# y written in the place of x, a reworked root chain, and the last channels packed in two pairs

## The chip, the cores and the metric

One core of one Trainium2 chip runs the kernel. The metric is device time in microseconds of one execution. The kernel before takes 917.46 us, the median of three runs (916.84 to 920.22).

## The reference

Two layers follow each other on x of shape 4 x 64 x 256 x 256, in float32.

```python
hx = _implicit_filter(z, Xw1, ..., t, deltas)          # 256 taps for each of 64 channels
hy = _implicit_filter(z, Yw1, ..., t, deltas)
k = jnp.einsum('ijk,imk->ijmk', hx, hy)[0]             # a separable 256 x 256 filter for each channel
y = irfft2(rfft2(x) * rfft2(k) / fft_size)[..., :L, :L]
x = y + x * bias[:, None, None]

x1 = transpose(x, (1, 0, 2, 3)).reshape(64, -1)
x1_s = x1[:, ::9]                                      # every ninth pixel
mean1 = mean(x1_s)
cov = x1_s @ x1_s.T / x1_s.shape[1] + 0.01 * eye(64)
deconv = _isqrt_newton_schulz(cov, 5)                  # Y, Z: T = 0.5(3I - ZY); Y = YT; Z = TZ
out = deconv @ (x1 - mean1)
```

The second layer needs the whole first layer before its first output pixel: the 64 x 64 inverse root depends on samples of every image and channel.

## The kernel before, in words

**Convolution.** The filter is separable and causal, so each channel is two multiplications by a triangular Toeplitz matrix, one for each axis. `steps` (L107) has 32 steps, each of eight channels (group g) of one image n; the last sixteen go image by image with groups 6 and 7. A step has four items of two channels. `group(first, second)` (L380) runs the first multiplication of one item and the second multiplication of the item two places before it as 80 interleaved matmuls on PE (L214). ACT then copies the first results from PSUM (L395), and DVE forms y = x * bias + PSUM (L398). `pack` gives DVE some copies under a mask (L312), which gather every ninth pixel of a finished step into `samp[n]`. `store` (L406) issues two DMAs of 256 KB on SP's queue, from the y tile to the DRAM tensors `y_d`. `load_x` (L100) brings x two steps ahead in four DMAs of 512 KB. `half_group` runs the first two and the last two items, for which only one of the two multiplications is left.

**Buffers.** The pool `big` holds four tiles of 16 KB a partition: two with tag "in" for x and two with tag "out" for y. `epool` has two more, `spool` the four `samp`, `tpool` three Toeplitz tiles: 13 tiles in all.

**Covariance.** `covariance(n)` (L320) is 58 matmuls over `samp[n]`. Those of images 0 to 2 stand between convolution groups. For the last four channels of the last step, 18 matmuls with a row-picking matrix (`pack_by_pe`, L288) take the place of the masked copies. Image 3's covariance follows.

**Root.** From L504 on: the 128 x 65 sum is folded to 64 x 64, A's Frobenius norm is taken through two square roots on ACT with a correction on DVE, A is scaled, and five Newton-Schulz rounds follow, each with up to three 64 x 64 products. PE, DVE and ACT alternate. W (the scaled root, repeated for both halves of the partitions) and `shift` (minus the root times the mean) come out.

**Apply.** Finished images are in `y_d` as 32 pieces of 2 MB. `load_y` (L345) brings a piece into one of 13 `homes` (L340), the tiles above, as soon as a tile's last use is over: `early` (L371) puts eight of these loads between convolution steps, five follow after the last store (L469). Each piece is multiplied by W on PE (L580), moved back to its tile by ACT (L585) and DVE (L588), which add `shift`, and written to `out` by DMAs on POOL's queue (L593): four of 512 KB for the first two and the last two pieces, one of 2 MB for the others. A home is loaded again when its piece has been written.

The order of instructions on PE, SP, DVE, ACT and POOL is the order of the program text inside `manual_schedule` (L419 to L470). The root and the apply stage stand outside it. Each queue runs in order; SP's and POOL's issue a DMA only when its buffers are free, and each reuses eight landing semaphores in turn.

Of the kernel before, what the change touches and what calls it, by code (L numbers as in the profile page):

```python
# [37 lines left out]
F32 = mybir.dt.float32  # L38
I32 = mybir.dt.int32
AF = mybir.ActivationFunctionType  # L40
ALU = mybir.AluOpType
# [7 lines left out]
CG = 8  # L49
# [16 lines left out]
def conv_whiten_kernel(ctx: ExitStack, tc: tile.TileContext, a: dict, out: bass.AP):  # L66
# [1 line left out]
    x = a["x"]  # L68

    const = ctx.enter_context(tc.tile_pool(name="const", bufs=1))  # L70
    big = ctx.enter_context(tc.tile_pool(name="big", bufs=2))
    epool = ctx.enter_context(tc.tile_pool(name="epool", bufs=2))
    spool = ctx.enter_context(tc.tile_pool(name="spool", bufs=NB))
    tpool = ctx.enter_context(tc.tile_pool(name="tpool", bufs=3))
# [7 lines left out]

    scratch = big.tile([P, 16, L], F32, tag="out", name="scratch")

    zw = scratch[0:EMB, 13:15, :].rearrange("p a w -> p (a w)")[:, 0 : L + P]
    nc.sync.dma_start(out=zw, in_=a["zw"])
# [18 lines left out]
    steps = [(g, n) for g in range(C // CG - 2) for n in range(NB)]  # L107
    steps += [(g, n) for n in range(NB) for g in range(C // CG - 2, C // CG)]

    x_tiles = [big.tile([P, CG, H2, L], F32, tag="in", name=f"x{u}") for u in range(2)]  # L110
    for c in range(0, CG, 2):
        load_x(x_tiles[0], *steps[0], c)

# [145 lines left out]

    def half_group(item, which):  # L260

        g, n, c, xt, yt, o1s = item
        jobs = []
        for u in range(2):
            banks = [
                psA.tile([P, L], F32, tag="psA", name=f"ph{which}_{g}_{n}_{c + u}_{m}")
                for m in range(H2)
            ]
            jobs.append((banks, (o1s[u] if which else xt[:, c + u]), toep[g][:, which, c + u, :]))
        toeplitz_alone(jobs, which)  # L270
        if which == 0:
            for u in range(2):
                o1s.append(o1pool.tile([P, H2, L], F32, tag="o1", name=f"o1_{g}_{n}_{c + u}"))
        for m in range(H2):
            for u in range(2):
                ps = jobs[u][0][m]
                if which == 0:
                    copy = nc.vector.tensor_copy if u else nc.scalar.copy
                    for to, fr in ((slice(0, HP), slice(HP, P)), (slice(HP, P), slice(0, HP))):
                        copy(o1s[u][to, m], ps[fr])  # L280
                else:
                    ch = g * CG + c + u
                    nc.vector.scalar_tensor_tensor(  # L283
                        yt[:, c + u, m], xt[:, c + u, m], bias[:, ch : ch + 1], ps,
                        ALU.mult, ALU.add,
                    )

    def pack_by_pe(g, n, yt, cs):  # L288
# [12 lines left out]
                )  # L301
        dst = samp[n][:, :, :, g * CG + cs.start : g * CG + cs.stop]
        nc.scalar.copy(dst[:, 0], pk[:, 0].rearrange("p c j -> p j c"))  # L303
        nc.vector.tensor_copy(dst[:, 1], pk[:, 1].rearrange("p c j -> p j c"))

    def pack_ops(g, n, yt, cs):
        def op(s):
# [12 lines left out]
    def covariance(n):  # L320
# [17 lines left out]


    homes = [  # L340
        {"t": (tpool, "toep"), "s": (spool, "samp"), "i": (big, "in"), "o": (big, "out"), "e": (epool, "extra")}[k]
        for k in "eetssitsoiots"
    ]

    def load_y(i):  # L345
# [22 lines left out]
            k = first + (part * 12 // 8 if g < C // CG - 2 else part)  # L368
            blocks[k // 4, k % 4 * 2] = (g, part)

    early = {(26, 4): 1, (26, 6): 1, (27, 4): 1, (28, 2): 1, (29, 6): 1, (31, 4): 2, (31, 6): 1}  # L371
    orders = [list(range(L // HP)), list(reversed(range(L // HP)))]

    def pack(time=math.inf):
# [5 lines left out]
    def group(first, second):  # L380

        units = []
        g1, n1, c1, x1, _, o1s1 = first
        g2, n2, c2, x2, y2, o1s2 = second
        for u in range(2):
            job2 = (bank(f"p2_{g2}_{n2}_{c2 + u}"), o1s2[u], toep[g2][:, 1, c2 + u, :])
            job1 = (bank(f"p1_{g1}_{n1}_{c1 + u}"), x1[:, c1 + u], toep[g1][:, 0, c1 + u, :])
# [4 lines left out]
        for u in range(2):  # L392
            o1 = o1pool.tile([P, H2, L], F32, tag="o1", name=f"o1_{g1}_{n1}_{c1 + u}")
            for to, fr in ((slice(0, HP), slice(HP, P)), (slice(HP, P), slice(0, HP))):
                nc.scalar.copy(o1[to], units[u][0][0][fr])  # L395
            o1s1.append(o1)
            ch = g2 * CG + c2 + u
            nc.vector.scalar_tensor_tensor(  # L398
                y2[:, c2 + u], x2[:, c2 + u], bias[:, ch : ch + 1], units[u][1][0],
                ALU.mult, ALU.add,  # L400
            )

# [1 line left out]
        store(second)  # L404

    def store(second):  # L406
        g, n, c, _, yt, _ = second
        last = (g, n) == steps[-1]
        for b in range(H2):
            row = b * C + g * CG + c  # L410
# [3 lines left out]
            )  # L414
        if last and c == CG // 2 - 2 or not last and c == CG - 2:
            todo.extend(pack_ops(g, n, yt, slice(0, c + 2)))

    engines = mybir.EngineType
    with tc.manual_schedule(  # L419
# [7 lines left out]
        for c in range(0, CG, 2):  # L427
            load_x(x_tiles[1], *steps[1], c)
        for i, (g, n) in enumerate(steps):
            xt = x_tiles[i % 2]  # L430
            yt = big.tile([P, CG, H2, L], F32, tag="out", name=f"y_{g}_{n}")
            for c in range(0, CG, 2):
                item = (g, n, c, xt, yt, [])
                if g == C // CG - 1 and n > 0 and c == 4:
                    covariance(n - 1)
                if len(pending) == 2:
# [4 lines left out]
                if i == 0 and c == 6:  # L441

                    fold = const.tile([P, C], F32, tag="fold", name="fold")
                    nc.vector.tensor_tensor(fold, ident[:, 0:C], ident[:, C:P], ALU.add)
                    twice = const.tile([C, 2, C], F32, tag="twice", name="twice")
                    for u in range(2):
                        nc.vector.tensor_copy(twice[:, u], ident[0:C, 0:C])

                j, cj = i - (c < 4), (c - 4) % CG
                if 0 <= j < len(steps) - 2:  # L450
                    load_x(x_tiles[j % 2], *steps[j + 2], cj)
                if (i, c) in blocks:
                    tg, part = blocks[i, c]
                    if part == 0:
# [2 lines left out]
                    load_toeplitz(toep[tg], tg, part // 4, part // 2 % 2, lo, lo + CG // 2)  # L457
                for _ in range(early.get((i, c), 0)):
                    load_next()
        g, n, c, xt, yt, _ = pending[0]  # L460
        for item in pending:
            half_group(item, 1)
            pack(1.0)
            store(item)

        pack()
        pack_by_pe(g, n, yt, slice(CG // 2, CG))
        covariance(NB - 1)
        while len(loaded) < len(homes):  # L469
            load_next()  # L470


    spare = {}
    for i in range(2):
        t = o1pool.tile([P, H2 * L], F32, tag="o1", name=f"chain{i}")
        for j in range(5):
            spare[5 * i + j] = t[0:C, 72 * j + 72 : 72 * j + 72 + C]
    ones = spare[9]
    nc.gpsimd.memset(ones, 1.0)  # L479
    i15 = spare[8]  # L480
    nc.vector.tensor_scalar(i15, ident[0:C, 0:C], 1.5, None, ALU.mult)
    spots = {"A": [0], "sq": [1], "Y": [2, 3], "T": [4, 5], "Z": [6, 7], "Zs": [1]}

    columns = [t[0:C, 440 + k : 441 + k] for k in range(H2 * L - 440)]

    def column():
        return columns.pop()

    def matrix(tag):
        spots[tag].append(spots[tag].pop(0))  # L490
        return spare[spots[tag][-1]]

    def product(lhsT, rhs, name):
        p = psA.tile([lhsT.shape[1], rhs.shape[1]], F32, tag="psA", name=name)
        nc.tensor.matmul(p, lhsT=lhsT, rhs=rhs, start=True, stop=True)  # L495
        return p

    def keep(p, name, tag):
        t = matrix(tag)
        nc.vector.tensor_copy(t, p)  # L500
        return t


    pd = product(fold, cov, "pd")  # L504
    A = matrix("A")
    nc.vector.scalar_tensor_tensor(A, ident[0:C, 0:C], EPS, pd[:, 0:C], ALU.mult, ALU.add)
    mean = column()
    nc.scalar.copy(mean, pd[:, C : C + 1])

    def root(v, name):  # L510

        s0 = column()
        nc.scalar.activation(s0, v, AF.Sqrt)  # L513
        r = column()
        nc.vector.reciprocal(r, s0)
        s1 = column()
        nc.vector.scalar_tensor_tensor(s1, v, r, s0, ALU.mult, ALU.add)
        s2 = column()
        nc.vector.tensor_scalar(s2, s1, 0.5, None, ALU.mult)
        return s2  # L520

    sq = matrix("sq")
    nc.vector.tensor_tensor(sq, A, A, ALU.mult)
    rowsum = column()
    nc.vector.tensor_reduce(rowsum, sq, AX.X, ALU.add)
    ssq = column()
    nc.vector.tensor_copy(ssq, product(ones, rowsum, "pn"))
    norm = root(ssq, "norm")
    rnorm = column()
    nc.vector.reciprocal(rnorm, norm)  # L530

    Y = matrix("Y")
    nc.vector.tensor_scalar(Y, A, rnorm, None, ALU.mult)
    Z = None
    for it in range(N_ITER):
        ZY = Y if Z is None else product(Z, Y, f"ZY{it}")
        T = matrix("T")
        nc.vector.scalar_tensor_tensor(T, ZY, -0.5, i15, ALU.mult, ALU.add)
        if it < N_ITER - 1:
            nextY = product(Y, T, f"YT{it}")  # L540
        if Z is None:
            newZ = T
        else:
            newZ = matrix("Z")
            nc.scalar.copy(newZ, product(T, Z, f"TZ{it}"))
        if it < N_ITER - 1:
            Y = keep(nextY, f"Y{it + 1}", "Y")
        else:
            snorm = root(norm, "snorm")
            rsnorm = column()  # L550
            nc.vector.reciprocal(rsnorm, snorm)
        Z = newZ

    Zs = matrix("Zs")
    nc.vector.tensor_scalar(Zs, Z, rsnorm, None, ALU.mult)
    twice = twice.rearrange("p u c -> p (u c)")
    W = o1pool.tile([P, H2 * L], F32, tag="o1", name="W")[:, 0:C]
    nc.vector.tensor_copy(W, product(twice, Zs, "pw"))
    shift0 = column()
    nc.vector.tensor_scalar(shift0, product(Zs, mean, "pz"), -1.0, None, ALU.mult)  # L560
    shift = const.tile([P, 1], F32, tag="shift", name="shift")
    nc.vector.tensor_copy(shift, product(twice, shift0, "ps"))


    halves = [slice(u * C, (u + 1) * C) for u in range(2)]
# [88 lines left out]
```

## Time and profile before

| What | Value |
|---|---|
| median of three runs | 917.46 us |
| profiled execution | 916.79 us, its span 914.9 us |
| PE busy | 789.4 us (86%) |
| DVE busy | 657.7 us (72%) |
| ACT busy | 479.1 us (52%) |
| DMA | 285.59 MB, mean 312 GB/s |
| first DMA to `out` | issued at 653.81 us |
| granted PE clock | 0.946 over the span |

The span splits in two. Up to about 620 us PE is busy without a break with the convolution, at full clock. After that PE's share falls, and the 16 DMA engines are busy to the end. Times in the trace count from the span's start. Two records of PE make one float32 matmul here. An idle engine that is not the bottleneck costs nothing.

### The profile page before, as it was taken

The page shows a single profiled execution, that of the slowest core. Times are in us where ns is not written, and L with a number is a line of the kernel's source. Part 1 is how long each engine was busy: PE and PEld are TensorE (multiplying, and loading weights), DVE is VectorE, ACT ScalarE, POOL GpSimd, SP SyncE. Part 2 cuts the span into 40 slices and gives each one's busy share as a digit, 9 for nine tenths or more (in the row PEclk, how much of TensorE's full clock was granted, in tenths as well). Part 3 has the DMA queues.
Part 4 walks back from the last instruction along what each step waited for, and adds up shares of the span by engine and source line. Part 5 has one row for each costly group of instructions (what it writes and reads, how often), then busy time and mean ns, then how long its engine had stood idle before and what let it go on. Part 6 is the DMA issues. An engine that isn't in the chain of part 4 may idle for free.

```text
span 914.9 us, 28251 instructions
## 1 busy us (share of the span) xinstructions
PE 789.4 (86%) x11876; PEld 633.3 (69%) x11876; DVE 657.7 (72%) x882; ACT 479.1 (52%) x791; POOL 31.8 (3%) x71
## 2 busy tenths in 40 slices
PE   8999999999999999999999999997877777765500
PEld 7999999999999999999999999996311111121100
DVE  3468776878687868786878666866699999986500
ACT  2545454545454545454545444540598888865400
POOL 3000000000000000000000000000110000000010
PEclk9999999999999999999999999998799999987655
DMA  4988788788788888888997897849999999999998
GB/s 155 295 264 262 247 262 265 232 269 260 249 263 262 248 256 264 258 253 275 285 275 227 310 378 289 300 139 406 422 418 426 428 429 429 430 430 427 433 433 333
DMA packets 117549, 285.59 MB, mean 312 GB/s; under 512 B 8973, under 2 KB 91312, under 8 KB 109744
## 3 DMA queue, kind: packets, MB, share of 16 engines
q1 hardware_dynamic: 110224, 216.09, 69.2%
q0 software_dynamic: 6336, 67.11, 17.3%
q8 instruction: 94, 1.54, 0.7%
q10 hardware_dynamic: 864, 0.60, 0.2%
q14 instruction: 31, 0.25, 0.1%
HBM read 149.35 MB, written 134.42 MB: 310 GB/s over the span
## 4 chain that ended last, share of the span: by engine, by line
PE 68%; issue 15%; DVE 14%; ACT 0%; DMA 0%; POOL 0%; POOLq 0%; DVEq 0%; ACTq 0%; SPq 0%
PE p L214 63%; DVE yi L588 12%; PE pc L326 2%; PE ph L246 1%; PE pk L294 1%; POOL out_dram L593 0%; DMA toep<-g_d 0%; DVE y L283 0%; PE busy L149 0%; PE po L580 0%; PE ZY L495 0%; PE YT L495 0%; PE pm L155 0%; DVE scratch L162 0%; ACT L513 0%
## 5 line engine op out<-in xcount | busy, mean ns | idle before, releaser
L214 PE MATMUL p<-toep,o 64*64 64x64 f32 (+3 forms) x5040 | 578.4, 284 | 0.0
L214 PE MATMUL p<-toep,x 64*64 64x64 f32 (+3 forms) x5040 | 578.3, 284 | 0.0
L214 PEld LDWEIGHTS p<-toep,x 64*128 64x128 f32 (+1 forms) x5040 | 534.2, 166 | 23.1
L214 PEld LDWEIGHTS p<-toep,o 64*128 64x128 f32 (+1 forms) x5040 | 535.4, 166 | 10.5 <-issue 0.2
L395 ACT COPY o<-p 64x512 f32<-64x512 f32 x504 | 292.4, 580 | 297.3 <-PE p L214 289.7
L312 DVE COPY_PREDICATED samp<-mask,y 128x448 f32<-128x448 int32 (+3 forms) x288 | 281.1, 976 | 6.6
L398 DVE SCALAR_TENSOR_TENSOR y<-x,bias,p 128x512 f32<-128x512 f32 x252 | 177.3, 744 | 138.4 <-PE p L214 130.2
L588 DVE TENSOR_SCALAR yi<-po,shift 64x512 f32<-64x512 f32 x256 | 192.1, 750 | 24.5 <-PE po L580 18.2
L580 PE MATMUL po<-yi,W 64*64 64x512 f32 x1024 | 153.2, 674 | 61.8 <-DVE yi L588 40.4
L585 ACT ACTIVATE yi<-po,shift 64x512 f32<-64x512 f32 x256 | 174.9, 683 | 43.7 <-PE po L580 36.7
L580 PEld LDWEIGHTS po<-yi,W 64*64 64x64 f32 x1024 | 36.8, 146 | 176.9 <-DVE yi L588 125.0
L593 POOL DMA_DIRECT2D out_dram<-yi x44 | 23.7, 538 | 263.5 <-DVE yi L588 100.6
L479 POOL MEMSET chain<- 64x64 f32 x1 | 0.1, 145 | 602.2 <-PE ph L246 602.2
L326 PEld LDWEIGHTS pc<-samp 128*64 128x64 f32 x464 | 14.4, 137 | 2.0 <-issue 1.2
L326 PE MATMUL pc<-samp 128*64 128x65 f32 x464 | 15.1, 223 | 0.5 <-ACT samp L303 0.4
L149 PE MATMUL busy<-idle 128*128 128x128 f32 x94 | 12.9, 301 | 0.0
L149 PEld LDWEIGHTS busy<-idle 128*128 128x128 f32 x94 | 12.4, 216 | 0.2 <-issue 0.2
L280 DVE COPY o<-ph 64x256 f32<-64x256 f32 x8 | 3.4, 422 | 9.1 <-PE ph L246 8.9
L294 PE MATMUL pk<-y,pick 128*128 128x112 f32 (+1 forms) x36 | 7.7, 389 | 2.5 <-DVE y L283 2.5
L334 DVE SCALAR_TENSOR_TENSOR cov<-pc,cov 128x65 f32<-128x65 f32 x4 | 0.9, 227 | 12.4 <-PE pc L326 12.4
L294 PEld LDWEIGHTS pk<-y,pick 128*128 128x128 f32 x36 | 7.2, 260 | 2.8 <-issue 2.7
L280 ACT COPY o<-ph 64x256 f32<-64x256 f32 x8 | 2.9, 367 | 10.0 <-DMA toep<-g_d 8.5
(81 smaller groups left out, 79.7 us busy)
## 6 DMA issues: line engine op xcount, KB each, us to landing
x<-in_x_dram SPq DMA_DIRECT2D x128, 512.0 KB, 5.3
y_d<-y SPq DMA_DIRECT2D x256, 256.0 KB, 3.5
yi<-y_d SPq DMA_DIRECT2D x32, 2048.0 KB, 15.7
out_dram<-yi POOLq DMA_DIRECT2D x28, 2048.0 KB, 44.6
out_dram<-yi POOLq DMA_DIRECT2D x16, 512.0 KB, 9.0
toep<-g_d SPq DMA_DIRECT2D x29, 256.0 KB, 6.2
toep<-g_d SPq DMA_DIRECT2D x29, 192.0 KB, 5.6
toep<-g_d SPq DMA_DIRECT2D x6, 128.0 KB, 3.1
```

The costliest lines, as they stand in the source:

```text
L149: nc.tensor.matmul(p, lhsT=idle[:, 0:P], rhs=idle[:, P : 2 * P], start=True, stop=True)
L214: mm = nc.tensor.matmul(ps[q : q + w, m, HP * k : L], lhsT=src[parts, k // 2, m * P + q : m * P + q + w], rhs=t[parts, : stop : -1] if k e ...
L246: mm = nc.tensor.matmul(ps[m][:, HP * k : L], lhsT=src[parts, k // 2, m * P : (m + 1) * P], rhs=t[parts, : stop : -1] if k else t[parts, : ...
L294: nc.tensor.matmul(pk[:, b, :, 0:nj], lhsT=pick[:, (s - b) % STEP, :], rhs=yt[:, cs, b, s : s + STEP * (nj - 1) + 1 : STEP], start=(s == 0 ...
L312: nc.vector.copy_predicated(dst, m, src)
L326: nc.tensor.matmul(pc[half], lhsT=samp[n][:, b, j, 0:C], rhs=samp[n][:, b, j, :], start=(b == 0 and j < 2), stop=(b == H2 - 1 and j >= NJ ...
L395: nc.scalar.copy(o1[to], units[u][0][0][fr])
L398: nc.vector.scalar_tensor_tensor(y2[:, c2 + u], x2[:, c2 + u], bias[:, ch : ch + 1], units[u][1][0], ALU.mult, ALU.add,)
L580: nc.tensor.matmul(po[u][halves[k]], lhsT=W[halves[u]], rhs=yt[halves[u], cols[k]], start=True, stop=True,)
L585: nc.scalar.activation(yt[halves[0], cols[k]], po[0][halves[k]], AF.Identity, bias=shift[halves[k]])
L588: nc.vector.tensor_scalar(yt[halves[1], cols[k]], po[1][halves[k]], shift[halves[k]], None, ALU.add)
L593: nc.gpsimd.dma_start(out=o[:, end - part : end], in_=yt[:, end - part : end])
```

## The change

**y in the place of x.** The pool `big` becomes `xpool` with four tiles of one tag. Step i uses tile i % 4 and DVE writes y over x. The x loads of step i + 2 are issued in step i at the same c, where before they were issued two items later. The homes are again 13 tiles, in another order, and `early` has nine loads at other places. The scratch of the filter network moves to `epool`.

**The root.** `whitening` takes the place of the old chain and stands inside `manual_schedule`. It forms the first round's T as a cubic in A with the reciprocal norm worked in, carries M and Q = TT in the rounds (two products on the chain in a round, where Z is formed beside it), makes the mean a 65th column of Z, and takes the second copy of the root from a T of 128 columns. `spin` issues matmuls whose result nothing reads. The square root's table is loaded in step 0 by an ACT instruction that writes a column of `bf`.

**The last channels.** `pack_by_pe` runs twice, for two channels each.

```diff
-    big = ctx.enter_context(tc.tile_pool(name="big", bufs=2))
+    xpool = ctx.enter_context(tc.tile_pool(name="xpool", bufs=4))
...
-    scratch = big.tile([P, 16, L], F32, tag="out", name="scratch")
+    scratch = epool.tile([P, 16, L], F32, tag="extra", name="scratch")
...
-    x_tiles = [big.tile([P, CG, H2, L], F32, tag="in", name=f"x{u}") for u in range(2)]
+    x_tiles = [xpool.tile([P, CG, H2, L], F32, tag="in", name=f"x{u}") for u in range(4)]
...
-        nc.vector.tensor_copy(dst[:, 1], pk[:, 1].rearrange("p c j -> p j c"))
+        copy = nc.vector.tensor_copy if cs.stop == CG else nc.scalar.copy
+        copy(dst[:, 1], pk[:, 1].rearrange("p c j -> p j c"))
...
-        for k in "eetssitsoiots"
+        for k in "eetssiistiits"
...
-    early = {(26, 4): 1, (26, 6): 1, (27, 4): 1, (28, 2): 1, (29, 6): 1, (31, 4): 2, (31, 6): 1}
+    early = {
+        (26, 4): 1, (27, 0): 1, (27, 4): 1, (28, 0): 1, (29, 6): 1, (30, 2): 1, (31, 2): 1, (31, 4): 1, (31, 6): 1
+    }
...
-                y2[:, c2 + u], x2[:, c2 + u], bias[:, ch : ch + 1], units[u][1][0],
+                x2[:, c2 + u], x2[:, c2 + u], bias[:, ch : ch + 1], units[u][1][0],
...
+    def spin(times):
+        p = psA.tile([P, P], F32, tag="psA", name=f"spin{len(spins)}")
+        spins.append(p)
+        for _ in range(times):
+            nc.tensor.matmul(p, lhsT=ident, rhs=ident, start=True, stop=True)
...
+    def whitening(i15, ones):
+        one_i15 = i15[:, 0]
+        pd = product(fold, cov, "pd")
...
+        nc.vector.scalar_tensor_tensor(A, ident[0:C, 0:C], EPS, pd[:, 0:C], ALU.mult, ALU.add)
...
+        nc.vector.tensor_tensor(sq, A, A, ALU.mult)
+        pa2 = product(A, A, "pa2")
+        pn = product(ones, sq, "pn")
...
+        nc.scalar.activation(A1b, A, AF.Copy, scale=-1.125)
+        nc.scalar.activation(A2a, pa2, AF.Copy, scale=-0.125)
+        nc.scalar.activation(A2b, pa2, AF.Copy, scale=0.75)
...
+        nc.vector.tensor_reduce(ssq, pn, AX.X, ALU.add)
+        nc.scalar.activation(s0, ssq, AF.Sqrt)
...
+        pa3 = product(A2a, A, "pa3")
+        spin(7)
+
+        nc.vector.reciprocal(r, s0)
+        nc.vector.tensor_scalar(r3, r, r, r, ALU.mult, ALU.mult)
+        nc.vector.tensor_scalar(h, r, 1.5, None, ALU.mult)
+        nc.vector.scalar_tensor_tensor(rn, r3, hm, h, ALU.mult, ALU.add)
...
+        nc.vector.scalar_tensor_tensor(U, pa3, rn_c, A2b, ALU.mult, ALU.add)
+        nc.vector.scalar_tensor_tensor(V, U, rn_c, A1b, ALU.mult, ALU.add)
...
+        nc.vector.scalar_tensor_tensor(T, V, rn_c, one_i15, ALU.mult, ALU.add)
+        nc.vector.tensor_scalar(M, V, rn_c, -2.0, ALU.mult, ALU.mult)
...
+        for k in range(1, N_ITER - 1):
+            pq = product(T, T, f"pq{k}")
+            if before is not None:
+                next_z(k - 1, before)
+            spin(1)
+            Q = Qs[k % 2]
+            nc.vector.tensor_copy(Q, pq)
+            pm = product(Q, M, f"pm_{k}")
...
+            if k < N_ITER - 2:
+                spin(1)
+                T, M = Ts[k % 2], Ms[k % 2]
+                nc.vector.scalar_tensor_tensor(T, pm, -0.5, one_i15, ALU.mult, ALU.add)
+                nc.vector.tensor_copy(M, pm)
...
+        pw = product(T, Z, "pw")
+        W = place(C)
+        nc.vector.tensor_scalar(W, pw[:, 0:C], rs, None, ALU.mult)
...
+        nc.scalar.activation(shift, pw[:, C : C + 1], AF.Copy, scale=nrs)
...
+                    nc.scalar.activation(bf[:, 0:1], samp[0][:, 0, 0, C : C + 1], AF.Sqrt)
...
-                j, cj = i - (c < 4), (c - 4) % CG
-                if 0 <= j < len(steps) - 2:
-                    load_x(x_tiles[j % 2], *steps[j + 2], cj)
+                if i + 2 < len(steps):
+                    load_x(x_tiles[(i + 2) % 4], *steps[i + 2], c)
...
-        pack_by_pe(g, n, yt, slice(CG // 2, CG))
+        for lo in range(CG // 2, CG, 2):
+            pack_by_pe(g, n, yt, slice(lo, lo + 2))
         covariance(NB - 1)
         while len(loaded) < len(homes):
             load_next()
+        W, shift = whitening(i15, ones)
```

## The prediction

> **What bounds the kernel now.** I read the page's slices first, then busy time by stage, the order of SP's and POOL's issues, and the chain that ended last. From the page:
>
> ```profile
> PE   8999999999999999999999999997877777765500
> DMA  4988788788788888888997897849999999999998
> GB/s 155 295 264 262 247 262 265 232 269 260 249 263 262 248 256 264 258 253 275 285 275 227 310 378 289 300 139 406 422 418 426 428 429 429 430 430 427 433 433 333
> ```
>
> PE is full until slice 26, DMA from slice 27 on. The slice between has 139 GB/s: just before the second bound begins, the DMA engines are half idle. Busy time by stage (PE, PEld, DVE, ACT, POOL, then PE clock, DMA share, GB/s) places that hole:
>
> ```profile
> 592.00:602.00 10.00, 10.00 (x172) 9.31 (x168) 9.40 (x12) 5.08 (x9) 0.00 (x0) 1.00 0.40 136
> 602.00:614.00 12.00, 12.00 (x270) 11.27 (x268) 4.81 (x8) 4.20 (x8) 0.00 (x0) 1.00 0.23 74
> 614.00:653.00 39.00, 29.14 (x283) 23.49 (x284) 23.25 (x57) 6.63 (x16) 0.14 (x1) 0.78 1.02 408
> 653.00:663.00 10.00, 10.00 (x73) 3.02 (x66) 9.69 (x14) 9.73 (x15) 3.40 (x7) 1.00 0.99 414
> 663.00:913.00 250.00, 139.74 (x942) 32.65 (x935) 181.07 (x242) 163.83 (x240) 20.29 (x38) 0.84 1.00 423
> ```
>
> From 592 to 614 us DMA idles 10 x 0.60 + 12 x 0.77 = 15.2 us. From 614 on it never stops. Since 614, SP's and POOL's timelines show why:
>
> ```profile
> 613.33 0.94 SPq L350 DMA_DIRECT2D yi<-y_d  x2
> 616.27 0.89 SPq L411 DMA_DIRECT2D y_d<-y  x2
> 617.25 0.42 SPq L350 DMA_DIRECT2D yi<-y_d  x1
> 619.97 5.20 SPq L411 DMA_DIRECT2D y_d<-y  x4
> 627.21 68.17 SPq L350 DMA_DIRECT2D yi<-y_d  x9
> 653.81 0.73 POOL L593 DMA_DIRECT2D out_dram<-yi  x1 [35.49 <-PE po L580]
> ```
>
> Eight pieces (three early ones, five of the last nine issues) and six stores are queued from 613.33 us: 8 x 2.097 + 6 x 0.262 = 18.35 MB. At the stage's 408 GB/s they need 45 us, to about 659 us. The first `out` write, at 653.81, therefore joins a queue that is still reading. So the root chain, though every engine waits for it, has some 5 us to spare. The end is set by bytes: from 613.33, 27 pieces in, 32 out and six stores are 125.3 MB, and 125.3 MB over the 300 us to 913 is 418 GB/s.
>
> **What the Trainium skill says.** *DMA: Bandwidth & Descriptors*, section Issuing engines are not separate DMA queues: DMAs of SP, ACT and POOL share the same 16 DMA engines. The trace agrees, since reads and writes together stay at 430 GB/s in the tail; the same page's Where 436 GB/s comes from gives a ceiling of 435, so no more rate is to be had and only idle time can go. *TensorE: Matmul & The Clock Gate*, What's actually happening: an idle window of some 3.4 us halves PE's clock. The trace agrees: 0.50 in most of the chain (0.60 over 636 to 650). The same page's LDWEIGHTS section says that a weight load costs by its columns; 128 columns take 260 ns on average in the `pk` group here, so halving the moving columns does not halve that.
>
> **Part 1: y in x, loads earlier.** The convolution keeps its matmuls, ACT copies, DVE operations and stores, and x and y have the same sizes: 0 us on PE. DVE writes over x only after both multiplications' turns; x was read two items before. The new order on SP: the x load of step i + 2 at c = 0 waits for the last masked copies of step i - 2, which run in that same group (3 copies, 3.0 us). Behind it on SP are that item's Toeplitz or early load and the next stores. At the start two x loads of step 2 now go ahead of the first stores, behind all Toeplitz loads of group 0 and step 1's x. Nobody on PE waits for these for less than a step, and x itself is needed eight items (some 36 us at the 4.5 us between store pairs) later. I cost this at 0; without that cover it is at most 3 us once a step.
>
> In exchange two tiles come free a step sooner. Read off SP's new order, piece 5 goes out behind the stores at (30,2) and piece 6 behind those at (31,2). The stores of those items were issued at 584.9 and 603.2 us. Both tiles are steps 28's and 29's, whose masked copies end in (30,0) and (31,0), about 2 us before. Before, pieces 5 and 6 went out at 613.33. They now fill the hole: 2 x 2.097 MB at 430 GB/s is 9.8 of the 15.2 idle us; the last two x loads (1.05 MB, 2.4 us) also leave 580 to 586 for earlier. Pieces 7 and 8 go at (31,4) and (31,6), 613.3 and 617.3 us; four follow the stores. So from 613.3 us there are 25 pieces to read, not 27. 4.19 MB less at 418 GB/s: **-10.0 us**, if DMA stays full from there. The queue in front of the first write is now 6 x 2.097 + 1.57 = 14.15 MB, done at 648 (408 GB/s) to 652 us (the old end near 662, when DMA starts on the writes, less 10).
>
> **Part 2: two pairs.** PE idled 2.54 us before `pk`, for DVE's last y. The first pair needs channels 4 and 5 only (their y is there at 620.7), so it can start when PE ends the convolution, 621.4 us. Cost before: 36 records in 7.67 us, 213 ns each, at a clock of about 0.79, so some 168 ns at full clock. Now 72 records. If a record's time goes with its columns, 6.1 us; if by weights and start, 72 x 0.168 = 12.1 us. I take 9 us: 621.4 to 630.4, against 631.6 before. DVE's ten masked copies end at 630.95 anyway, plus two 64 x 64 fillings (2 x 0.18) ahead of the last copy, and covariance 3 cannot start before. So about 0, bounds -0.5 and +2.5; the covariance's 3.7 us stay, and the sum over them ends at 635.7 as before.
>
> **Part 3: the chain.** Before, from the chain that ended last:
>
> ```profile
> 636.86 1.28 ACT L513
> 641.38 0.47 PE YT L495 x2
> 641.85 0.23 PE TZ L495 x2
> 642.10 0.21 ACT chain L545
> 642.36 0.49 PE ZY L495 x2
> 642.87 0.23 DVE chain L538
> ```
>
> One round on the path is ZY, DVE, YT, TZ, ACT with five gaps: 642.10 to 643.86, 1.76 us. From 635.98 to W at 648.76 is 12.8 us; then PE also makes `ps` before the first `po` at 649.62. The table load of 1.28 us leaves the path for step 0, where ACT is half idle (5.08 of 10 us), so 0 there. New path after the covariance, with full-clock products of 0.34 (the `pd` row), DVE steps of 0.22 and gaps of 0.03: pd and A 0.6; sq, pn, row sum 1.05; Sqrt on ACT 0.24; r, r3, h, rn 0.8; U, V, T 0.75. Sum 3.45. The seven spins are 14 records of 137 ns (the `busy` group: 94 in 12.9 us), 1.9 us in PE's queue behind pa3, ahead of pq1: they end at 3.7, so T waits 0.25. Three rounds of pq, spin or Q copy (0.28), pm, T (0.25): 1.25 each, and Z's products put 0.3 more in the second and third; last pz and spin 0.6 less what T hides, pw of 128 columns 0.5, W 0.25. Sum 3.7 + 3.75 + 0.6 + 1.25 = 9.3 us. W at 635.7 + 9.3 = 645.0, and `po` can start at once: 4.6 us sooner. At half clock products rise by 0.13, spins double: +4 us, W at 649. The first write follows `po` by 653.81 - 649.62 = 4.2 us: 649.2, or 653.2.
>
> **What is late next.** The chain saves nothing by itself; it keeps DMA fed, since the reads now end at 648 to 652. At 649.2 the first write joins as they end. But the queue is then empty, and the apply stage makes 512 KB each 1.55 us (POOL's issues), 338 GB/s, until the first home is written and can be loaded again some 7 us later. Loss 7 x (1 - 338/430) = 1.5 us, and 0.5 for the wait on the first whole-piece write. **+1.5 to +3, taken +2.0** less the 1 us of the same kind in 653 to 700 before: +1.0.
>
> **Sum.** -10.0 + 0 + 1.0 = -9.0. On the profiled execution 916.79 - 9.0 = 907.8; its span plus 1.9 us outside. The median of the runs is 0.67 above it, so **908.5 us**.
>
> **Rivals.**
>
> A, no gain from the moved loads: if tiles 28 and 29 are still held at (30,2) and (31,2), SP blocks and the six pieces become eight again; the chain alone then moves the first write within a queue that is busy anyway. 917 us. For it: before, the queue absorbed everything to 659. Against: the program's order on DVE frees the tiles one item earlier.
>
> B, the chain becomes the bound: the clock stays at half, so W comes at 649 to 651 instead of 645. The first write then passes 653 to 655 and DMA runs dry by 1 to 3 us more: 910 to 913. For it: 0.50 through this stage before.
>
> C, slower: PE at half clock from the convolution's end, and a `pk` record that does not shrink with its columns. 72 records at 2 x 168 ns take 24.2 us, from 621.4 to 645.6; copies 0.6, covariance 2 x 3.7, chain 13.3: W at 667, first write at 671. Reads end at 652, so DMA stands still for 19 us: -10 + 19 + 1 = +10, 927 us. It decides once W passes 657, where 9 us of standing still eat the gain. Against: PE has no 2.5 us pause ahead of `pk` any more, after which the clock fell to 0.5 before, and the covariance ran at 1.0.
>
> **How the numbers follow.** The first case 0.76 (own range 905.5 to 911.5), B 0.09, A 0.08, C 0.07. Half a per cent (4.6 us) is about what a measurement can tell from no change: below 912.9 is faster. B reaches that line, two thirds of it clearly faster: 0.76 + 0.06 = 0.82; same 0.03 + 0.08 = 0.11; slower 0.07. The low end, 904, is the case without the +1 loss and with a read queue drained at 388 rather than 418 GB/s (10.8 us), plus 1.5 for other idle time in 560 to 592; the high end, 913.5, takes B in.
>
> **What would show it.** Right: DMA share between 592 and 614 near 0.75; two single `yi` issues between 585 and 605; no pause of DMA over 1 us between 614 and the end; first `out` issue near 649; PE clock 1.0 through the chain; tail unchanged at about 430 GB/s. Wrong: PE waiting for x or DVE inside the convolution, so that it ends after 622; `pk` ending after 634; W after 650; a DMA share below 0.9 between 645 and 660.

## The result, and the profile after

The changed kernel takes 912.36 us, the median of seven runs (910.57 to 915.02), against 917.46 for the kernel before in the same comparison: a ratio of 0.9939, 95% interval 0.9922 to 0.9957. It is faster by 5.1 us. The likeliest case had said 908.5, so a gain of 9 us; the sign and the range were right, the size was not. The profiled execution took 911.48 us, its span 909.6 us.

The page of the kernel after, busy tenths and rate in 40 slices:

```profile
PE   8999999999999999999999999999977777764500
DMA  4988888798788878879997899779999999999998
GB/s 152 306 275 271 248 258 246 252 272 259 244 263 262 247 234 258 275 239 275 276 281 253 262 395 360 261 275 366 398 386 429 431 430 429 432 427 432 431 430 340
```

The slice with 139 GB/s is now at 275: the hole ahead of the second bound is half filled. But three slices after it stand at 366 to 398, where before all stood over 400. The windows by stage (PE, PEld, DVE, ACT, POOL, then PE clock, DMA share, GB/s), kernel after:

```profile
592.00:602.00 10.00, 10.00 (x178) 9.46 (x176) 9.35 (x12) 5.44 (x10) 0.00 (x0) 1.00 0.78 276
602.00:614.00 12.00, 12.00 (x264) 11.10 (x264) 4.79 (x8) 3.69 (x7) 0.00 (x0) 1.00 0.73 265
614.00:653.00 39.00, 35.51 (x401) 28.88 (x398) 29.05 (x66) 10.67 (x28) 1.47 (x3) 1.00 0.98 385
653.00:663.00 10.00, 9.59 (x58) 2.58 (x56) 9.69 (x14) 9.73 (x15) 3.20 (x6) 1.00 0.91 337
663.00:908.00 245.00, 133.59 (x926) 30.19 (x918) 177.96 (x238) 160.69 (x236) 19.22 (x36) 0.85 1.00 422
```

Against the same windows of before, at 614 us the kernel is ahead by 10 x (276 - 136) + 12 x (265 - 74) = 3.69 MB, 8.8 us at 418 GB/s. It then gives back 39 x (408 - 385) = 0.90 MB and 10 x (414 - 337) = 0.77 MB, together 4.0 us. That leaves 4.8 us of lead at 663; the span is 5.3 us shorter. (By the DMA records of the two traces the kernel was 0.18 MB, 0.4 us, ahead at 592 us already, which closes the sum.) So the gain is where the prediction had put it, and nearly half is lost again between 614 and 663 us. SP's and POOL's issues in that stretch:

```profile
588.25 0.49 SPq L351 DMA_DIRECT2D yi<-y_d  x1
606.52 0.45 SPq L351 DMA_DIRECT2D yi<-y_d  x1
615.44 0.45 SPq L351 DMA_DIRECT2D yi<-y_d  x1
619.57 0.47 SPq L351 DMA_DIRECT2D yi<-y_d  x1
622.37 4.60 SPq L414 DMA_DIRECT2D y_d<-x  x4
627.50 10.57 SPq L351 DMA_DIRECT2D yi<-y_d  x4
650.61 0.73 POOL L628 DMA_DIRECT2D out_dram<-yi  x1 [27.05 <-DVE yi L623]
```

The two single issues that fill the hole are there. (Their data are in DRAM by then because the last eight steps go image by image. The description of the kernel before says sixteen, but `steps` has 6 x 4 + 4 x 2.) The last of the 13 early pieces lands at 653.72 us (662.65 before), while the first write to `out` is issued only at 650.61 us and lands at 655.01. What leads up to it, from the chain that ended last of the kernel after (start, duration, what):

```profile
632.75 0.62 DVE samp L313
633.46 0.22 ACT samp L303
...
633.96 3.73 PE pc L327 x116
...
646.45 0.38 PE pw L443 x2
646.85 0.29 DVE chain L536
647.19 1.16 PE po L615 x8
```

The root takes what was said, from the end of the covariance's sum (637.71 + 0.23) to W (647.14) 9.2 us. It starts 2 us later than said, because DVE's masked copies end that much later, and PE's packing (done at 631.94) is not what the covariance waits for.

### The profile page after: what moved, and what is told of

It reads as the page before. It is cut to its first block, busy times and chain, and to the rows that moved or that the text cites. A ratio compares the mean times of both kernels' runs of the same rounds, so it can differ in the third digit from the quotient of the medians.

```text
span 909.6 us, 28298 instructions
## 1 busy us (share of the span) xinstructions
PE 788.3 (87%) x11934; PEld 634.0 (70%) x11934; DVE 658.3 (72%) x882; ACT 480.2 (53%) x798; POOL 31.8 (3%) x71
## 4 chain that ended last, share of the span: by engine, by line
PE 68%; DVE 13%; issue 7%; another core or an unknown queue 5%; DMA 4%; POOL 1%; ACT 1%; SPq 0%; ACTq 0%; POOLq 0%; DVEq 0%
PE p L214 64%; DVE yi L623 11%; DMA yi<-y_d 3%; PE pc L327 2%; PE ph L246 1%; ACT yi L620 1%; DVE samp L313 1%; PE po L615 1%; DMA mask<-in_mask_dram 1%; POOL pick L130 1%; POOL out_dram L628 0%; DVE x L283 0%; DMA toep<-g_d 0%; PE spin L428 0%
## 5 line engine op out<-in xcount | busy, mean ns | idle before, releaser
L313 DVE COPY_PREDICATED samp<-mask,x 128x448 f32<-128x448 int32 (+3 forms) x288 | 281.2, 976 | 6.7
L401 DVE SCALAR_TENSOR_TENSOR x<-x,bias,p 128x512 f32<-128x512 f32 x252 | 177.3, 743 | 140.6 <-PE p L214 140.1
L615 PE MATMUL po<-yi,chain 64*64 64x512 f32 x1024 | 149.0, 649 | 62.4 <-DVE yi L623 42.2
L615 PEld LDWEIGHTS po<-yi,chain 64*64 64x64 f32 x1024 | 34.7, 140 | 175.8 <-DVE yi L623 131.5
L294 PE MATMUL pk<-x,pick 128*128 128x56 f32 (+1 forms) x72 | 8.3, 292 | 0.0
L294 PEld LDWEIGHTS pk<-x,pick 128*128 128x128 f32 x72 | 8.1, 192 | 0.1
```

Of the source, the lines that this page charges most:

```text
L294: nc.tensor.matmul(pk[:, b, :, 0:nj], lhsT=pick[:, (s - b) % STEP, :], rhs=yt[:, cs, b, s : s + STEP * (nj - 1) + 1 : STEP], start=(s == 0 ...
L313: nc.vector.copy_predicated(dst, m, src)
L401: nc.vector.scalar_tensor_tensor(x2[:, c2 + u], x2[:, c2 + u], bias[:, ch : ch + 1], units[u][1][0], ALU.mult, ALU.add,)
L615: nc.tensor.matmul(po[u][halves[k]], lhsT=W[halves[u]], rhs=yt[halves[u], cols[k]], start=True, stop=True,)
```

## The experiments

The theory after the first comparison: with the old loads the early reads last to 663 us and hide the root; with the new ones they end near 653 us, close to the first write to `out`, and then the time of that write sets the end. Every run below was compared with the kernel before on the same chip. "Reads end" is the landing of the 13th early piece in the profiled execution.

| Run | Median, us | Ratio to before, interval | Profiled, us | First out issue | Reads end |
|---|---|---|---|---|---|
| before | 917.46 | | 916.79 | 653.81 | 662.65 |
| root and pairs only | 917.03 | 0.9993 [0.9983, 1.0003] | 916.42 | 650.34 | 663.69 |
| that, root 4.1 us longer | 917.11 | 0.9994 [0.9987, 1.0002] | 916.14 | 653.28 | 663.50 |
| loads only | 916.15 | 0.9983 [0.9976, 0.9990] | 917.05 | 655.46 | 653.62 |
| after | 912.36 | 0.9939 [0.9922, 0.9957] | 911.48 | 650.61 | 653.72 |
| after, again | 912.19 | 0.9938 [0.9923, 0.9953] | 912.76 | 651.96 | 654.03 |
| after, again (2) | 912.52 | 0.9944 [0.9930, 0.9958] | 913.20 | 652.57 | 654.86 |
| Toeplitz piece first | 913.16 | 0.9953 [0.9938, 0.9968] | 912.94 | 651.61 | 651.95 |
| Toeplitz load ahead of x | 912.21 | 0.9948 [0.9931, 0.9966] | 912.53 | 651.83 | 651.76 |
| one packing | 912.13 | 0.9943 [0.9932, 0.9955] | 912.13 | 651.52 | 652.08 |
| root 4.1 us longer | 914.52 | 0.9968 [0.9956, 0.9979] | 912.52 | 651.91 | 652.09 |
| pause filled | 910.88 | 0.9935 [0.9921, 0.9949] | 910.88 | 650.42 | 652.16 |
| both mends | 911.14 | 0.9924 [0.9909, 0.9940] | 911.79 | 651.13 | 654.63 |
| pause filled, root shorter | 909.53 | 0.9917 [0.9900, 0.9934] | 908.85 | 647.66 | 651.22 |

**The two halves of the change.** Root and pairs alone:

```diff
-        pack_by_pe(g, n, yt, slice(CG // 2, CG))
+        for lo in range(CG // 2, CG, 2):
+            pack_by_pe(g, n, yt, slice(lo, lo + 2))
...
+        W, shift = whitening(i15, ones)
```

> The old buffers and the old order of loads, with the new root and the two packing pairs alone. Theory (bytes moved before 614 us set the end, the chain's length does not): W comes near 645 us instead of 648.8, the first out write is issued near 650 us, but it joins a queue that is reading until some 659 us, and the time is 917 us within 1 us. Rival (the end follows the first out write): 913 to 914 us.

Buffers and loads alone:

```diff
-    big = ctx.enter_context(tc.tile_pool(name="big", bufs=2))
+    xpool = ctx.enter_context(tc.tile_pool(name="xpool", bufs=4))
...
-        for k in "eetssitsoiots"
+        for k in "eetssiistiits"
```

> The new buffers and the new order of loads alone, with the old root and one packing of four channels. Theory: the lead in bytes at 614 us is kept (share of DMA over 592 to 614 near 0.75), but reads end near 652 us and the first out write comes only near 655 us, so DMA stands still for some 3 us: 913 to 915 us. Rival (the gain comes from the shorter chain, the moved loads being hidden anyway): 917 us. If the late end of the convolution comes from the new order of loads and not from root or packing, PE's last convolution record ends after 623 us here too, and at 621.4 us in the kernel with the new root alone.

Measured: no difference that can be told (0.9993) and a gain of 0.17%, where both together bring 0.6%. The first came out as the theory said, though `po` started only at 646.92 us. The second gained less than expected (916.15, not 913 to 915). Its windows show what happens when the reads end ahead of the root; behind them stand those of the old loads with a root lengthened by 4.1 us. Loads only:

```profile
648.00:653.00 5.00, 3.82 (x21) 2.13 (x24) 0.99 (x5) 0.20 (x1) 0.00 (x0) 0.50 0.68 292
653.00:658.00 5.00, 5.00 (x36) 1.54 (x32) 4.42 (x6) 4.16 (x7) 1.26 (x2) 0.68 0.25 103
658.00:663.00 5.00, 5.00 (x41) 1.54 (x36) 4.83 (x8) 4.88 (x8) 1.59 (x3) 1.00 0.83 329
```

Old loads, new root, 4.1 us longer:

```profile
648.00:653.00 5.00, 4.62 (x45) 2.43 (x47) 2.12 (x4) 2.17 (x4) 0.00 (x0) 1.00 1.00 426
653.00:658.00 5.00, 5.00 (x40) 1.36 (x32) 4.86 (x7) 4.88 (x8) 1.97 (x4) 1.00 1.00 427
658.00:663.00 5.00, 5.00 (x29) 1.36 (x26) 4.84 (x8) 4.85 (x8) 1.96 (x4) 1.00 0.98 405
```

With the loads only, the rates fall short of 430 GB/s by 5 x (138 + 327 + 101) = 2.83 MB, 6.6 us at full rate: the lead is lost again as standing DMA. With the old loads they stay at 405 or more, although the first write, at 653.28, is about as late as before (653.81). The kernel after has 388, 361 and 313 GB/s there, a loss of 2.7 us.

**The root made longer, with either loads.** Fifteen unread products, 30 records, before the last product, once in the changed kernel and once with the old loads:

```diff
         Z = Zs[(N_ITER - 2) % 2]
+        spin(15)
         pw = product(T, Z, "pw")
```

> The changed kernel with fifteen more unread products, 30 records of 137 ns, so 4.1 us, in front of the last product of the root. Theory (the moved loads have taken away the queue that covered the root: reads end near 654 us and the first out write is issued at 650.6 to 652 us, so that every later us of W is lost): first out write near 655 us, time 3 to 4 us above the changed kernel's, 915.3 to 916.3 us. Rival (the queue of reads still covers the root, as it did in the kernel before): no change, 912.3 us within 0.6.

> The kernel with the old loads and the new root, with fifteen unread products (4.1 us) ahead of the last product of the root. Theory (with the old loads the queue of reads lasts until 663 us and covers the root): the first out write moves from 650.3 to some 653.7 us and the time stays at 917.0 us within 0.7, although the same 4.1 us cost 2.3 us with the new loads. Rival (the first out write sets the end whatever the loads): 919.5 to 921 us.

With the old loads the time does not move (917.11 against 917.03), though the first write is issued 2.9 us later (653.28 against 650.34). With the new ones it rises by about 2.2 us, against the 912.2 to 912.5 of the unaltered kernel; these are runs of other batches, but the means of the eight runs and of the 17 differ by 1.9 us with a standard error of 0.5. That is what the theory says: the same addition is free under a queue of reads and costs where it has gone. How long a root the old queue would cover is not shown: with the old loads the lengthened root brought the first write back only to where it had been before (653.81), not beyond it. The cost was less than the 3 to 4 us expected. One part is seen in the profiles: `pd` to `pw` grew by 11.74 - 8.39 = 3.35 us, not 4.1; it may be that some of the unread products ran while PE would have waited. The profiled execution with the new loads, 912.52 us, is also the lowest of its eight, so it does not show the cost that the median has; there the convolution ended at 621.7 us and the covariance ran at full clock, and its first write at 651.91 was no later than in the unaltered kernel's second profile (651.96, 912.76 us).

**What an earlier first write is worth.** The table's profiled executions with the new loads (ten with an unshortened root) fit a line of 1.18 us for each us of the first out issue, 1.03 without the far point of loads only. That is an association between executions, not a test. To test it with an earlier write, the kernel with the pause filled (`spin(7)` ahead of the last covariance, shown further below) leaves out one of its Newton-Schulz rounds:

```diff
-N_ITER = 5
+N_ITER = 4
...
-                for _ in range(2):
+                for _ in range(4):
                     steps_rs.pop(0)()
```

> The kernel with the filled pause (seven unread products ahead of the last covariance), and with one round of the iteration to the inverse root left out, so that its root is a less exact one: a probe of what an earlier first out write is worth. W comes some 1.3 us sooner and the first out write is issued near 649.2 us, which is where the prediction had put it. Theory (over ten profiles with the new loads the execution's time went as 1.0 to 1.2 us for each us of the first out write): profiled execution near 909.6 us, median 1 to 1.6 us below the kernel with the filled pause, 909.3 to 909.9 us. Rival (below 650 us the reads, which end at 652 to 654 us, set the end): 910.9 us within 0.5.

POOL's first issue in it:

```profile
647.66 0.73 POOL L629 DMA_DIRECT2D out_dram<-yi  x1 [26.88 <-DVE yi L624]
```

The first write came 2.76 us earlier than with the pause filled alone (0.7 of it from an earlier covariance), and the execution was 2.03 us shorter, 0.74 for each us; the medians differ by 1.35 us. The first write came at 647.66 us and not at the 649.2 expected. The rival, that below 650 us the reads set the end, fell. Why each us is worth less than by the line above is not shown. Between the two profiles, a first write at the predicted 649.2 gives 910.0 us by a straight line: an estimate from one execution of each kernel. The prediction had 907.8 for it.

**A hole that does not matter.** In the changed kernel DMA has 215 GB/s in 612 to 616 us. A piece issued earlier fills that hole:

```diff
-        for k in "eetssiistiits"
+        for k in "eetssiitsiits"
...
-        (26, 4): 1, (27, 0): 1, (27, 4): 1, (28, 0): 1, (29, 6): 1, (30, 2): 1, (31, 2): 1, (31, 4): 1, (31, 6): 1
+        (26, 4): 1, (27, 0): 1, (27, 4): 1, (28, 0): 1, (29, 6): 1, (30, 2): 1, (31, 2): 2, (31, 4): 1
```

> The changed kernel, but the early piece that waited for samp 2 changes places with the one that goes into the first spare Toeplitz tile, and both x tiles are followed by it at once: 13 pieces as before, the Toeplitz one issued four channels earlier. Theory (each us in which DMA stands still before the end of the reads is lost at the end): the hole at 614 to 616 us (134 GB/s) is filled, which is 1.3 us; 909.5 to 911.5 us. Rival (the apply stage alone sets the end, the reads having slack): 912.4 us within 0.5.

Its windows:

```profile
612.00:616.00 4.00, 4.00 (x104) 3.87 (x99) 3.62 (x5) 2.32 (x4) 0.00 (x0) 1.00 1.03 422
648.00:653.00 5.00, 4.81 (x45) 1.79 (x48) 3.60 (x6) 3.79 (x7) 0.73 (x1) 1.00 0.36 147
```

The changed kernel in the same batch:

```profile
612.00:616.00 4.00, 4.00 (x108) 3.77 (x106) 3.29 (x4) 2.32 (x4) 0.00 (x0) 1.00 0.57 219
648.00:653.00 5.00, 4.62 (x46) 1.70 (x49) 3.39 (x6) 3.45 (x6) 0.73 (x1) 1.00 0.75 315
```

The hole is filled (422 instead of 219) and comes back at 648 to 653 us (147 instead of 315). There are 13 homes: once they are full, DMA has nothing to do until W is there, and loading them sooner only makes that wait longer. No gain was measured: 913.16 us, even a little above the 911.9 to 912.9 of the rival, with an interval that overlaps that of the unaltered kernel. The theory that each standing us before the end of the reads costs one fell.

**The two pairs, and PE's pause.** One packing of four channels again, and, in another run, seven unread products behind the two pairs:

```diff
-        for lo in range(CG // 2, CG, 2):
-            pack_by_pe(g, n, yt, slice(lo, lo + 2))
+        pack_by_pe(g, n, yt, slice(CG // 2, CG))
```

```diff
             pack_by_pe(g, n, yt, slice(lo, lo + 2))
+        spin(7)
         covariance(NB - 1)
```

> The changed kernel with one packing of four channels, as before, in the place of two pairs. Theory (the last covariance waits for DVE's masked copies and not for PE's packing; with the pairs PE is done 2.0 us early, pauses, and the covariance then runs at a clock near 0.57 in most executions, 5.29 us instead of 3.71): PE ends the packing within 0.4 us of the masked copies, the covariance takes 3.7 us, W comes no later than with the pairs, and the time is 911 to 912.5 us. Rival (the pairs bring the covariance forward): W 1 to 2 us later, 913.3 to 914.5 us.

> The changed kernel with seven unread products, 1.9 us, on PE between the second packing pair and the last covariance, in the 2.0 us in which PE waits for the masked copies. Theory (that pause lets the clock fall, and the root's start with it; the root now bounds): the covariance takes 3.71 us at clock 1.0 in every execution, W near 647 us, time 0.5 to 1.5 us below the changed kernel's, 910.8 to 911.8 us. Rival (the clock falls for another reason, or the root has slack): covariance 5.3 us or time 912.3 us within 0.4.

PE's timeline, the changed kernel again (its second profile):

```profile
623.46 8.28 PE L294 MATMUL pk<-x,pick 128*128 128x58 f32 x72
633.74 5.29 PE L327 MATMUL pc<-samp 128*64 128x65 f32 x116 [2.01 <-ACT samp L303]
```

One packing:

```profile
624.34 7.69 PE L294 MATMUL pk<-x,pick 128*128 128x116 f32 x36 [2.57 <-DVE x L283]
632.43 3.71 PE L327 MATMUL pc<-samp 128*64 128x65 f32 x116 [0.40 <-ACT samp L303]
```

Pause filled:

```profile
629.68 1.77 PE L428 MATMUL spin<-ident 128*128 128x128 f32 x14
631.88 3.71 PE L327 MATMUL pc<-samp 128*64 128x65 f32 x116 [0.43 <-ACT samp L303]
```

The pairs bring the covariance's start forward by 0.5 us only (631.88 against 632.43, with convolutions that end 0.1 us apart), and PE waits 2.0 us for the masked copies. In six of the eight profiles with that pause the covariance then takes 5.05 to 6.40 us; in two (the first profile after among them) and in all six in which PE waits some 0.4 us, it takes 3.71. The clock of the second profile, by windows:

```profile
634.00:634.50 0.50, 0.50 (x22) 0.50 (x18) 0.00 (x0) 0.00 (x0) 0.00 (x0) 0.79 1.26 459
634.50:637.00 2.50, 2.50 (x52) 2.50 (x49) 0.00 (x0) 0.00 (x0) 0.00 (x0) 0.50 0.97 410
637.00:638.00 1.00, 1.00 (x29) 1.00 (x28) 0.00 (x0) 0.00 (x0) 0.00 (x0) 0.65 1.03 426
```

The clock is halved from about 634.3 to 637.7 us, while PE is full. One packing costs as much as the pairs (912.13 us). Filling the pause gave 910.88 us, the 0.5 to 1.5 us expected, but its interval and that of the unaltered kernel overlap.

Both profiles hide part of what they have to show, for the clock was halved again, later, inside the root. With the pause filled:

```profile
640.00:645.00 5.00, 5.00 (x31) 3.74 (x30) 2.23 (x13) 0.78 (x4) 0.00 (x0) 0.81 1.00 426
645.00:650.00 5.00, 4.62 (x23) 1.78 (x26) 1.90 (x4) 1.78 (x4) 0.00 (x0) 0.50 0.94 400
```

By the clock records it was halved from 643.12 to 649.95 us here, from 643.02 to 649.85 with one packing, from 641.75 to 648.58 with the root shorter, and from 647.82 to 651.23 with the Toeplitz load ahead. `pd` to `pw` then took 9.1 us with the pause filled and 9.7 with one packing, instead of 8.4, and in all four the first write followed `po` by 4.2 to 4.3 us instead of 3.4. So the first writes at 650.42 and 651.52 us would have come some 1.6 and 2.2 us sooner at full clock (an estimate from these differences). No pause of PE over 0.46 us stands in those roots; what halved the clock there is open.

**The convolution's late end.** It ended at 623.74 us after, 621.38 before. The Toeplitz loads stood under suspicion, since from 299.9 to 302.0 us SP waits for the masked copies ahead of one of them (its issue is at 302.38 us, 300.19 before):

```diff
-                if i + 2 < len(steps):
-                    load_x(x_tiles[(i + 2) % 4], *steps[i + 2], c)
                 if (i, c) in blocks:
...
                     load_toeplitz(toep[tg], tg, part // 4, part // 2 % 2, lo, lo + CG // 2)
+                if i + 2 < len(steps):
+                    load_x(x_tiles[(i + 2) % 4], *steps[i + 2], c)
```

> The changed kernel once more, unaltered. If the late end of the convolution (623.74 against 621.38 us) belongs to the change, PE's last convolution record again ends after 623 us and the time is 911 to 913.5 us. If it was chance of that one execution, it ends by 622 us and the profiled span is 1.5 to 2.5 us shorter than 909.6.

> The changed kernel with the x load of an item issued behind that item's Toeplitz load instead of ahead of it. Theory (the x load at channel 0 waits some 2.2 us on SP for the masked copies, and holds the Toeplitz loads queued behind it, which PE then meets late near 304 and 310 us): PE has no pause of its own in the convolution, the issues of Toeplitz loads near 302 us come 2 us earlier, the convolution ends by 622.2 us instead of 623.5, everything after it comes as much sooner, and the time is 1 to 2 us below the changed kernel's 912.3, that is 910.3 to 911.3 us. Rival (the pauses come from elsewhere): the convolution ends after 623 us and the time is 912.3 us within 0.5.

> The changed kernel once more, beside the next two on one chip, for the convolution's end, which lay at 623.3 to 623.7 us in four profiles and at 621.4 to 621.8 in four others, and for the covariance, which took 3.7 us in some and 5.3 in others. Theory (the moved x load holds the Toeplitz loads up to where PE just meets them or not): if PE pauses near 304 to 310 us here, the kernel with the Toeplitz load ahead does not in the same batch. Rival (chance of the execution): both or neither pause. Time 912.3 us within 0.6.

> Both mends together: the Toeplitz load ahead of the x load, and seven unread products in PE's 2.0 us before the last covariance. Theory (with the reads in by 654 us the first out write sets the end): convolution ends by 621.9 us, covariance 3.7 us, first out write by 650.6 us, time 910 to 911.3 us. Rival (the mends do not matter): 912.3 us within 0.5.

In its first repetition the unaltered kernel ended at 623.5 us, as if the late end belonged to the change. With the Toeplitz load ahead, that load was issued at 299.93 us and the convolution ended at 621.5 us, but in that batch the three kernels without this mend ended at 621.7 to 621.8 too; the time stayed at 912.21 us, with a covariance of 6.40 us. In the last batch the convolution ended at 624.3 us with the mend and 624.4 without. The waits of PE in two profiles of the unaltered kernel, after and then after again (2) (who waited for what, us in total, times, longest):

```profile
PE p L214 <- issue: 0.7, 2, 0.4
```

```profile
PE p L214 <- issue: 1.7, 2, 1.0
```

The pauses lie near 304 and 310 us in the first, at 203 and 281 in the second, and at 43 and 477 with both mends, and the records name no releaser. So the Toeplitz load does not explain the late end as a whole. Near 304 to 310 us it is not cleared: counted by groups of 160 records, five of the nine profiles with the new loads and without the mend lose 0.4 to 1.5 us against the usual 9.15 in the group that begins at 301 to 304 us, but none of the two with the mend and none of the three with the old loads. With four of the nine losing nothing there, two are too few to tell. With the old loads three profiles ended between 621.4 and 621.9, with the new ones eleven between 620.9 and 624.4. Whether the new order makes such pauses likelier, or these executions had them by chance, stays open.

**Both mends together.** They gave 911.14 us, a ratio of 0.9924 to before: faster than the kernel before by 0.6 to 0.9%, and 1.4 us under the unaltered change in the same batch, with overlapping intervals. The time is as expected, but not by the way expected: the convolution ended at 624.3 us and not by 621.9, and the first write came at 651.13 us and not by 650.6. Both kernels with the pause filled (910.88 and 911.14 us) lie below all three medians of the unaltered one (912.19 to 912.52), and the Toeplitz load alone gave 912.21, so the part that did it, if any, is the filled pause.

## Why the prediction was right and wrong

**What bounds the kernel now**: right. Bytes behind a full DMA queue set the end, and the root had slack under them: with the old loads it cost nothing to move the first write from 650.3 to 653.3 us. The 5 us to spare beyond 653.8 were not tried.

**Part 1**: mechanism right, two terms off. Pieces 5 and 6 went out at 588.25 and 606.52 us (the second 1.5 us behind the stretch named), and the DMA share over 592 to 614 was 0.78 and 0.73, near the 0.75 named. The lead gained over these windows was 8.8 us where -10.0 was summed. And the 0 on PE was wrong for this execution: 2.4 us, -0.4 to 3.0 us over the profiles, which the text itself had listed as a sign of error. It passes to DVE's masked copies, covariance and W.

**Part 2**: "about 0" was right for the packing, but not for its neighbour. The masked copies release the covariance, as said; that PE would therefore stand still for 2.0 us, and the covariance run at half clock behind it, was not drawn from that. It costs 1.3 to 2.7 us where it happens, which it did not in the first profile after.

**Part 3**: right in size, 9.2 us for 9.3, at full clock, from the end of the sum over the covariance. That sum had ended at 635.97 us before; the 635.7 from which the prediction counts is the end of the matmuls, 0.3 us too early. With a late start W came at 647.1 instead of 645.0, and the first write, 3.4 us behind `po` instead of 4.2, at 650.61 instead of 649.2. The 4.2 had been read from an execution whose clock was halved until 652.33 us.

**What is late next**: this is the step that failed in size. +1.0 was booked; the windows show 2.1 us lost in 614 to 653 and 1.8 in 653 to 663. The second is the term that was priced by the apply stage's 338 GB/s: 337 were measured, but over 10 us and not 7 (in two parts of 361 and 313 GB/s, so that the close agreement is in part luck). The wrong move was to take 1 us off for the same loss before (663 to 700 us still has 416 GB/s after, 420 before, so that loss stayed), and to count DMA as full from 614 on (it moved 134 GB/s in 614 to 616 us). By the estimate from the two probes, a first write at 649.2 is worth 910.0 and not 907.8: 2.2 of the 3.7 us by which the profiled execution missed; the other 1.5 fits the first write at 650.61.

**The range**: its low end of 904 does not come out of its own terms: 917.5 - 10.8 - 1.5 is 905.2. The result did not come near it.

**The rivals**: A fell (the homes were free in time). C was far: W came at 647 to 649 us in the changed kernel's profiles, not past 657, though its ingredient, a halved clock behind a pause, was real at another place. B named the time (910 to 913) and, in part, the cause: the root became a bound, in the three profiles of the changed kernel by its start and not by its own clock. In those of one packing and of the filled pause its own clock was halved too.

## What to carry to other kernels

When a transfer is moved forward, look for what it had been hiding: here each half of the change alone gained under 0.2%, and both 0.6%, because the queue covered the root, and the writes start when the root is done. Count the buffers that can be filled before the next stage starts; beyond that count an earlier load bought nothing here, whatever hole it filled. And when an engine is sped up ahead of a wait that it does not end, price the pause that it will make, its clock included.

## What the runs showed of the hardware that was not expected

A pause of PE of 2.0 us was followed by a halved clock in six of eight profiles, for 3.4 us in five of them and for 6.8 us in the sixth (the Toeplitz load ahead). In the six profiles with a wait of only 0.4 us there, the covariance ran at full clock. The kernel before had shown it already: behind the convolution its longest pauses of PE are 2.54 us, ahead of `pk`, and 2.35 us, from 637.5 to 639.8 us. The clock was halved 1.1 us after the first had ended, and within the second.

The clock records also tell the six profiles from the two. In each execution the clock changes only at instants that lie whole multiples of 3.41 us apart, and where these instants lie differs from one execution to the next. In the six, such an instant fell between 1.0 us after the pause had begun and 0.7 us after it had ended, and there the clock was halved. In the two others the nearest instants lay 0.1 to 0.2 us after the pause had begun and 1.5 us after it had ended, and the clock stayed whole. Eight cases are few. What else counts is not shown: with one packing the clock fell 1.6 us after the end of a pause of 2.57 us.

The Trainium skill, *TensorE: Matmul & The Clock Gate*, What's actually happening, speaks of an idle window of some 3.4 us and says that the window runs freely. These traces agree with a free window of that length. But the pause that sufficed was shorter than the window: in the 3.41 us ahead of each of the six falls PE still worked for 1.4 us or more.
